# A GRU over 128 steps on one core: a one-column product of zeros ahead of two kinds of products, weight loads at most two at a time, r's biases after all of r's products, and one block's weight sums moved forward

## The chip, the core and the metric

The kernel runs on one core of a Trainium2 chip, in one launch. Its engines: TensorE (PE, with its weight loads listed apart as PEld), VectorE (DVE), ScalarE (ACT), GpSimd (POOL) and SyncE (SP), which here only issues DMAs. The metric is the device time of one execution in microseconds (us), the median over the runs; lower is better. All data are float32, except where a tile is called bfloat16.

## The reference

`x` is (64, 128, 512), 64 sequences of 128 steps of 512 features; the initial state is `cond_1024` (64, 512). Each gate has a weight of 1024 x 512 (the upper half for x, the lower for the state) and a bias.

```python
do_prop = ((t + 1) % 4 == 0) & (t < T - 1)
def step(h, inp):
    x_t, prop = inp
    comb = jnp.concatenate([x_t, h], axis=-1)
    z = jax.nn.sigmoid(comb @ Wz + bz)
    r = jax.nn.sigmoid(comb @ Wr + br)
    comb2 = jnp.concatenate([x_t, r * h], axis=-1)
    h_cand = jnp.tanh(comb2 @ Wh + bh)
    h_new = (1.0 - z) * h + z * h_cand
    h_next = jnp.where(prop, jnp.tanh(h_new @ Wp + bp), h_new)
    return (h_next, h_new)
_, ys = jax.lax.scan(step, h0, (xs, do_prop))
return x + transpose(ys)
```

So each step has a candidate product (with `r * h`), and after every fourth step but the last the state goes through one more product, called the projection here.

## The kernel before, in words

**Tiles.** The 64 sequences are two lanes of 32 (`h` = 0 and 1, `S` = 2, `V` = 32). The 512 features are four chunks of 128; PE's array is used as four column groups of 32 columns (`part(q)`, q = 0 to 3), each with the 32 sequences of a lane as its weights. `four_tiles` (L279) issues one product on each of the four groups; a product with all 512 features is four of them, 16 instructions ("x16" in the profile). The moving data are the weights of the network, 128 columns (or 192 in the products on x).

**Two kinds of work on PE.** The recurrent products of step t need the state of step t-1: the r and z gates (`wrz`, L279, lines with bank_B<-wrz,ht or bank_A<-tr,ht), then the candidate (`wc`), then, after every fourth step, the projection (`wp`). The products on x (`wx`, L708) need no state. They are done for four steps at a time (a group), by a scheme that replaces eight block products by seven, blocks 1 to 7, made of sums of weights and of inputs; the sums of weights (`sums_w`) are made once, at the start. The units of these products are put by `fill` between the recurrent ones, so that PE has work while DVE and ACT compute the gates. All of it is in an order written out ahead, engine by engine; each engine does its instructions in that order and waits at each for the semaphores of what it reads.

**A step's chain.** r's products on PE, sigmoid on ACT (L1031, bank_A), `r * h` on DVE (L1146), its transposition on DVE (L275, tile `rhT`), the candidate's products on PE into bank_B (lane 0) and bank_C (lane 1), tanh on ACT, the new state on DVE (L1263, L1264). ACT has copied the x part into the bank ahead of the candidate's products (`seed_h`, L1007), and the bias `bp` ahead of the projection's (L1152). So the first product of a candidate waits for two engines: DVE for rhT, ACT for the bank.

**The start.** SP issues, in this order: x of steps 0 and 1, the x half of r's weight in three parts (`load_wx`, L162), x of step 2, the x halves of z's and the candidate's weight in two parts each (L162), then, in `later_loads`, the recurrent weights of r and z (`load_w`, L141, tile `wrz`), x of step 3 and of group 1, `wc`, x again, and after that `wp`. POOL issues the loads of the biases (tile `stage`) and of the initial state (cond). The first three steps' products on x are done plainly (`plain_gate`), with the biases as small bfloat16 products (`bias_products`, L600, from `thirds`, the three bfloat16 parts of the biases, which DVE makes in L229 to L234). Before there is data, PE runs products on zeros (`idle`, L259). DVE joins and transposes x into xT (L353), later sums the recurrent weights (L972). POOL makes the sums of weights of blocks 4 to 7 by `sum_inner` (L307 and L312, tiles sums_w and wx), one task for each block, after a first sum called "left".

The places that the change touches, cut to their core:

```python
for ks in (range(0, 1), range(1, 2), range(2, K)):
    for t in range(2):
        plain_gate(t, R, ks, bias=ks[-1] == K - 1)
later_loads()
join_x(0, 2)
plain_gate(2, R, range(K), bias=True)
...
for i in (6, 5, 4, 7):
    task(f"inner{i}", lambda i=i: [sum_inner(i, Gp), sum_left(i, Gp)], "left")
```

Of the kernel before, what the change touches and what calls it, by code (L numbers as in the profile page):

```python
# [10 lines left out]
BF16 = mybir.dt.bfloat16  # L11
# [7 lines left out]
def kernel(  # L19
# [14 lines left out]
    nc = tc.nc  # L34
    B, T, D = x.shape
    H = h0.shape[1]
    P = 128
    S = 2
    V = B // S
    NQ = P // V  # L40
    J = H // NQ
    U = J // 2
    C = 2
    K = D // P
# [4 lines left out]
    R, Z, H_ = range(3)  # L49
    assert V * NQ == P and D == H and J == P and T % 8 == 0  # L50

    const = ctx.enter_context(tc.tile_pool(name="const", bufs=1))
# [4 lines left out]
    ctx.enter_context(tc.manual_schedule())  # L57


    zeros = two.tile([P, 4 * J], BF16, tag="e_sb", name="zeros")  # L60
    nc.vector.memset(zeros, 0.0)
    ident = const.tile([3 * V, 3 * V], F32, name="ident")
# [10 lines left out]
    wx = const.tile([P, K, 3, H], F32, name="wx")  # L73
# [18 lines left out]
    gates_in = (Wr, Wz, Wh)  # L92
# [12 lines left out]
    def part(q):  # L105
        return slice(q * V, (q + 1) * V)
# [9 lines left out]
    row = (bank["B"], bank["C"])  # L116
# [7 lines left out]
    def load_x(tile_, t0, n, later=None):  # L124
        for h in range(S):
            for q in (0, 2, 1, 3):
# [9 lines left out]
                else:  # L136
                    later.append(run)

    def load_w(wt, w):
        for k0 in (0, 2):  # L140
            nc.sync.dma_start(  # L141
                out=wt[:, k0 : k0 + 2, :],
                in_=w.rearrange("(p k) n -> p k n", k=K)[:, k0 : k0 + 2],
            )

    both_queues = (nc.sync, nc.scalar)
# [12 lines left out]
            )  # L159

    def load_wx(i, k0, k1):
        nc.sync.dma_start(  # L162
            out=wx[:, k0:k1, i, :],
            in_=gates_in[i][:D].rearrange("(p k) n -> p k n", k=K)[:, k0:k1],
        )

    lands = {}
# [34 lines left out]
    for h in range(S):  # L202
        nc.gpsimd.dma_start(
            out=h_rows[:, h, :],
            in_=h0[ts(h, V), :].rearrange("b (q j) -> q b j", q=NQ),
# [62 lines left out]
    def plain_order(v):  # L268
        return v.rearrange("p (e k) -> p k e", k=K)

    def state_order(v):
        return v.rearrange("p (k e) -> p k e", k=K)
# [4 lines left out]
    def four_tiles(region, left, rhs, start=False):  # L277
        for q in range(NQ):
            nc.tensor.matmul(  # L279
                region[part(q)],  # L280
                lhsT=left,
                rhs=rhs(q),
                start=start,
                stop=True,
                skip_group_check=True,
            )


    def tick(ns):
        nonlocal clock  # L290
        clock += ns
# [223 lines left out]
    def flush(pending, late=0, most=99):  # L515
        n = 0
        while pending and n < most:
            b, j = pending.pop(0)
            n += 1
            late += 560  # L520
            b.out(j)
            b.out_at[j] = clock + late
            if b.finished():
                flying.remove(b)
                did.add(b.name)
        poll()
        return n
# [14 lines left out]
    def fill(n, eager=False, soon=True):  # L542
        nonlocal doing, owed
        drip(DRIP)
        n, owed = n + owed, 0
        while n > 0:
            if queue:
                unit, cost, end = queue.pop(0)
                unit()
                tick(cost * UNIT)  # L550
                n -= cost
                if end is not None:
                    end()
                poll()
                continue
            if doing is None:
                best = pick()
                if best is None or best[0] > clock + 400:
                    owed = n
                    return  # L560
                b, j = best[1:]
                b.left.remove(j)
                doing = b, j, b.units(j)
            b, j, us = doing
            us.pop(0)()
            tick(UNIT)
            n -= 1
            if not us:
                doing = None
                b.made_at[j] = clock  # L570
                (at_dve if j in (3, 7) else at_act).append((b, j))
                if soon:
                    flush(at_act, 300)
                    if eager:
                        flush(at_dve, 300)

    def x_left(t, h, k):
        g, j = divmod(t, Q4)
        c0, s0 = divmod(k, C)
        return xT[g][:, j][:, c0, s0 * B + h * V : s0 * B + (h + 1) * V]  # L580

    def plain_bank(t, h):
        return row[h] if t == 0 else xb[2 * (t % 2 if t > 3 else t == 2) + h]

    def plain_gate(t, i, ks, bias=False):
        for h in range(S):
            region = plain_bank(t, h)[:, ts(i, J)]
            for k in ks:
                four_tiles(
                    region,  # L590
                    x_left(t, h, k),
                    lambda q: wx[:, k, i, ts(q, J)],
                    i == R and k == 0,
                )
            if bias:
                bias_products(region, slice(i, i + 1))

    def bias_products(region, which):
        for q in range(NQ):
            nc.tensor.matmul(  # L600
                region[part(q)],
                lhsT=picks[:, q],
                rhs=thirds[:, which],
                start=False,
                stop=True,
                skip_group_check=True,
            )
# [220 lines left out]
    def poll():  # L828
        again = True
        while again:  # L830
            again = False
            for n, (name, run, after, step) in enumerate(todo):
                if steps_done >= step and all(a in did for a in after):
                    del todo[n]
                    run()
                    did.add(name)
                    again = True
                    break
# [135 lines left out]
    def first_sums(v):  # L974
        turn(ht[:, A11 : A12 + 1].rearrange("p n v -> p (n v)"), v)
# [29 lines left out]
    def seed_h(t, lane, h):  # L1005
        have_sums(t)
        nc.scalar.copy(  # L1007
            row[lane][:, 2 * J : 3 * J].rearrange("p (n u) -> p n u", n=C), G[t][:, h, :, H_]
        )
# [8 lines left out]
    PLAIN = T - 4  # L1018
# [54 lines left out]
    def full(region, lT, w):  # L1073
        for k in range(K):
            four_tiles(region, lT[:, ts(k, V)], lambda q: w[:, k, ts(q, J)])
# [13 lines left out]
    }  # L1089

    def tile_(tag, t, pool=one):
        return pool.tile([P, S, J], F32, tag=tag, name=f"{tag}_{t}")

# [41 lines left out]
    def step(t, h_old, v_1):  # L1135
# [73 lines left out]
        if last:  # L1209
# [5 lines left out]
            for h in range(S):  # L1215
                nc.vector.scalar_tensor_tensor(
                    out=kept[:, h], in0=z_[:, h], scalar=1.0, in1=h_h[:, h],
# [6 lines left out]
        else:  # L1224
            nc.vector.scalar_tensor_tensor(
                out=keep, in0=z_ps, scalar=1.0, in1=h_old, op0=ALU.subtract, op1=ALU.mult
# [19 lines left out]
        def candidate(h):  # L1246
            region = row[h][:, 2 * J : 3 * J]
            full(region, rhT[:, h], wc)
            tick(FULL)
            c, z_h = cand[:, h], z_ps[:, h]  # L1250
            if last:
                nc.scalar.activation(c, region, AF.Tanh)
                nc.vector.tensor_mul(z_h, c, z_h)
                o = xr[g][:, j, h, :]
                nc.vector.tensor_add(o, z_h, o)
                for q in (0, 2, 1, 3):
                    way = both_queues[q // 2] if h else nc.sync
                    way.dma_start(out=out[ts(h, V), t, ts(q, J)], in_=o[part(q)])
                return
            nc.scalar.activation(state_order(c), plain_order(region), AF.Tanh)  # L1260
            if t + 1 < T and not prop:
                seed_h(t + 1, h, h)
            nc.vector.tensor_mul(z_h, c, z_h)  # L1263
            nc.vector.tensor_sub(h_new[:, h], z_h, keep[:, h])  # L1264

        candidate(0)
        if prop:
            pT = tile_("rhT", f"{t}p")
# [17 lines left out]
        for h in range(S):  # L1286
            fill(next(places), eager)
            flush(at_act, 300)
            full(row[h][:, :J], pT[:, h], wp)
            tick(FULL)  # L1290
            nc.scalar.activation(state_order(h_next[:, h]), plain_order(row[h][:, :J]), AF.Tanh)
            seed_h(t + 1, h, h)
            if h == 0:
                flush(at_dve, 300, 1) or join_next()
                first_sums(h_next[:, 0])
                join_next() or flush(at_dve, 1000, 1)
            else:
                second_turn(h_next[:, 1])
# [35 lines left out]
    idle(4)  # L1334
    for ks in (range(0, 1), range(1, 2), range(2, K)):
        for t in range(2):
            plain_gate(t, R, ks, bias=ks[-1] == K - 1)
    later_loads()
    join_x(0, 2)
    plain_gate(2, R, range(K), bias=True)  # L1340
    spread(bank["E"], slice(0, 2))
    spread(bank["A"], slice(2, 3))
    h_init = tile_("h", "init", two)
# [35 lines left out]
    task("raw12_1", lambda: sum_raw12(1), ("join", 1, 0), ("join", 1, 1))  # L1379
    task("left", lambda: [sum_outer_1(Gp), did.add("outer1")], "plain3")  # L1380
    task("raw34_1", lambda: sum_raw34(1), ("join", 1, 2), ("join", 1, 3))
    for i in (6, 5, 4, 7):
        task(f"inner{i}", lambda i=i: [sum_inner(i, Gp), sum_left(i, Gp)], "left")

    def pair(a, p1, p2, n):
# [27 lines left out]
    h, v_1 = h_init, None  # L1413
    for t in range(T):
        if t == 1:
            load_group(3)
        h, v_1 = step(t, h, v_1)
# [39 lines left out]
```

## Time and profile before

| | |
|---|---|
| runs | 1255.95 us median of 3 (1255.64 to 1255.97) |
| the profiled execution | 1254.05 us, its span 1252.3 us |
| PE busy | 1224.6 us, 98% of the span, 37576 instructions |
| DVE, ACT, POOL busy | 901.9, 683.9, 916.5 us |
| PE busy from 60 to 1200 us | 1131.88 us of 1140.00 |
| PE busy from 5 to 60 us | 47.23 us of 55.00 |

The span runs from the first to the last thing that the profiler recorded; the execution's time holds a little besides. A line such as "139.99 0.41 PEld L279 LDWEIGHTS bank_B<-wc,rhT ... x16 [0.16 <-ACT bank_A L1031]" gives the start, the length, the engine and line of a run of like instructions, and in brackets how long the engine had been idle before it and what ended that. Where an instruction waits for two engines, one alone is named. Rows of stretches give the length, then the busy time (and count) of PE, PEld, DVE, ACT and POOL, the granted TensorE clock (1.00 is full, 0.50 half), the DMA engines' busy share and GB/s.

### The profile page before, as it was taken

To read this page: it belongs to the slowest core of one execution; us is meant where nothing else is said; L and a number is where in the kernel's file an instruction comes from. 1 tells how busy PE (TensorE), PEld (TensorE's weight loads), DVE (VectorE), ACT (ScalarE), POOL (GpSimd) and SP (SyncE) were. 2 spreads that over 40 slices of the span, in tenths; PEclk is the share of its full clock that TensorE was granted. 3 is DMA by queue.
4 is the path that set the end of the run, shared out by engine and by line. 5 is a ranking of instruction groups with operands and counts; after the bars stand their busy time and mean duration, and the time that the engine had idled before them with its cause. 6 is when DMAs were issued, how large, how long until landed. Compare 5 with 4: busy or idle time off the path is not lost.

```text
span 1252.3 us, 84837 instructions
## 1 busy us (share of the span) xinstructions
PE 1224.6 (98%) x37576; PEld 1121.4 (90%) x37576; DVE 901.9 (72%) x2964; ACT 683.9 (55%) x2086; POOL 916.5 (73%) x1046
## 2 busy tenths in 40 slices
PE   7999999999999999999999999999999999999987
PEld 6789999999999999989889999998899999999977
DVE  5667777777777777777767777777777777777664
ACT  1345555555555555555555565555555555555554
POOL 1698686877868778686876868778687786868751
PEclk8999999999999999999999999999999999999999
DMA  7203222212222112222212221212222122222111
GB/s 241 82 17 74 52 53 57 54 48 51 56 57 56 46 49 54 57 52 54 53 47 50 53 65 47 59 46 50 57 54 49 50 55 56 52 57 51 50 48 48
DMA packets 98686, 72.26 MB, mean 58 GB/s; under 512 B 13028, under 2 KB 94576, under 8 KB 98320
## 3 DMA queue, kind: packets, MB, share of 16 engines
q1 hardware_dynamic: 97888, 66.54, 20.8%
q8 instruction: 295, 4.83, 1.6%
q14 instruction: 71, 0.58, 0.2%
q0 software_dynamic: 256, 0.14, 0.0%
q10 hardware_dynamic: 176, 0.16, 0.0%
HBM read 25.63 MB, written 16.78 MB: 34 GB/s over the span
## 4 chain that ended last, share of the span: by engine, by line
PE 94%; issue 1%; POOL 1%; DVE 1%; ACT 1%; DMA 0%; DVEq 0%; POOLq 0%; ACTq 0%
PE x L708 39%; PE bank_B L279 20%; PE bank_C L279 15%; PE bank_A L279 13%; PE bank_E L279 5%; PE x L279 2%; DMA stage<-in_L_cond_bh_dram 0%; POOL wx L312 0%; POOL sums_w L312 0%; ACT bank_A L1031 0%; POOL sums_w L307 0%; DVE xT L353 0%; DVE wrz L972 0%; POOL stage L193 0%; ACT gx L819 0%
## 5 line engine op out<-in xcount | busy, mean ns | idle before, releaser
L307 POOL TENSOR_TENSOR mb<-mb,mb 128x768 f32<-128x768 f32 x167 | 304.8, 1833 | 168.6 <-ACT mb L752 74.8
L708 PE MATMUL x<-sums_w,s 128*32 128x192 f32 x2880 | 178.5, 326 | 0.0
L307 POOL TENSOR_TENSOR xr<-xr,h 128x256 f32<-128x256 f32 x127 | 111.0, 874 | 83.1 <-DMA xr<-in_x_dram 48.0
L279 PE MATMUL bank_B<-wrz,ht 128*32 128x128 f32 x4000 | 168.3, 273 | 2.5 <-issue 1.7
L279 PE MATMUL bank_A<-tr,ht 128*32 128x128 f32 x3936 | 163.7, 273 | 0.5 <-DVE bank_B L1182 0.5
L279 PE MATMUL bank_B<-wc,rhT 128*32 128x128 f32 x4096 | 139.5, 274 | 3.0 <-ACT bank_B L1152 0.5
L279 PE MATMUL bank_C<-wc,rhT 128*32 128x128 f32 x4096 | 139.4, 273 | 0.1
L279 PEld LDWEIGHTS bank_B<-wrz,ht 128*32 128x32 f32 x4000 | 128.7, 110 | 10.4 <-issue 6.4
L279 PEld LDWEIGHTS bank_B<-wc,rhT 128*32 128x32 f32 x4096 | 110.4, 109 | 25.3 <-ACT bank_A L1031 20.3
L279 PEld LDWEIGHTS bank_A<-tr,ht 128*32 128x32 f32 x3936 | 124.9, 110 | 8.0 <-DVE bank_B L1182 4.8
L819 ACT COPY gx<-mb 64x384 f32<-64x384 f32 x248 | 126.4, 510 | 3.0
L708 PE MATMUL x<-sums_w,o 128*32 128x192 f32 x1920 | 121.3, 326 | 1.2 <-issue 1.2
L279 PEld LDWEIGHTS bank_C<-wc,rhT 128*32 128x32 f32 x4096 | 118.5, 110 | 0.3 <-ACT bank_C L1152 0.3
L708 PEld LDWEIGHTS x<-sums_w,s 128*32 128x32 f32 x2880 | 106.0, 110 | 5.7
L1189 DVE TENSOR_TENSOR bank_C<-bank_A,gx 128x256 f32<-128x256 f32 x123 | 53.2, 432 | 72.9 <-PE bank_A L279 72.9
L1146 DVE TENSOR_TENSOR rh<-bank_A,h 128x128 f32<-128x128 f32 x192 | 56.0, 292 | 50.0 <-ACT bank_A L1031 43.3
L738 ACT COPY x<-x 128x384 f32<-128x384 f32 x108 | 49.9, 462 | 76.4 <-PE x L708 76.4
L307 POOL TENSOR_TENSOR mb<-mb 128x768 f32<-128x768 f32 x47 | 86.3, 1835 | 2.5
L1031 ACT ACTIVATE bank_A<-bank_B 128x128 f32<-128x128 f32 x123 | 32.2, 262 | 102.2 <-DVE bank_C L1189 99.6
L275 DVE STREAM_TRANSPOSE rhT<-rh 128x128 f32<-128x128 f32 x256 | 79.8, 312 | 9.0
L1264 DVE TENSOR_TENSOR h<-bank_E,keep 128x128 f32<-128x128 f32 x254 | 74.1, 292 | 15.2
L752 ACT COPY mb<-x 128x384 f32<-128x384 f32 x108 | 51.7, 479 | 57.4 <-PE x L708 53.8
(884 smaller groups left out, 3100.1 us busy)
## 6 DMA issues: line engine op xcount, KB each, us to landing
gx<-mb SPq DMA_DIRECT2D x248, 96.0 KB, 2.2
xr<-in_x_dram SPq DMA_DIRECT2D x248, 64.0 KB, 2.9
out_dram<-xr SPq DMA_DIRECT2D x248, 64.0 KB, 1.8
wx<-in_L_cond_Wz_dram SPq DMA_DIRECT2D x2, 512.0 KB, 6.0
wx<-in_L_cond_Wh_dram SPq DMA_DIRECT2D x2, 512.0 KB, 7.1
wrz<-in_L_cond_Wr_dram SPq DMA_DIRECT2D x2, 512.0 KB, 9.4
wrz<-in_L_cond_Wz_dram SPq DMA_DIRECT2D x2, 512.0 KB, 9.6
wc<-in_L_cond_Wh_dram SPq DMA_DIRECT2D x2, 512.0 KB, 5.7
```

The source lines that it names most:

```text
L275: nc.vector.transpose(out=dst, in_=src)
L279: nc.tensor.matmul(region[part(q)], lhsT=left, rhs=rhs(q), start=start, stop=True, skip_group_check=True,)
L307: nc.gpsimd.tensor_add(o, a, b)
L708: nc.tensor.matmul(v[part(2 * h + c)], lhsT=left[:, ts(h, V)], rhs=right[:, c::2], start=j in (1, 5) and m == 0 and n == 0, stop=True, ski ...
L738: nc.scalar.copy(self.a, self.u)
L752: nc.scalar.copy(self.block(1, 0), runs(self.u))
L819: (ready, lambda h=h: (nc.scalar.copy(to(h, h), of(h, h)), one_done(clock + 1000)))
L1031: nc.scalar.activation(gate_out(dst), gate_in(lane, i), AF.Sigmoid)
L1146: nc.vector.tensor_mul(rh[:, h], r_ps[:, h], h_old[:, h])
L1189: nc.vector.tensor_add(row[1][:, : 2 * J].rearrange("p (n j) -> p n j", n=2), bcast(u_ps), G[t][:, 1, :, :2].rearrange("p n g u -> p n (g ...
L1264: nc.vector.tensor_sub(h_new[:, h], z_h, keep[:, h])
```

## The change

Four edits:

1. A tile `nil` of zeros (bfloat16, 128 x 34) is set once. `touch(v)` issues a product of it, with one moving column, on column group 0, added to what is in the bank (`start=False`), so that it changes nothing there. It stands ahead of the candidate's first product in steps 1 to T-5 (123 times) and ahead of the projection's first product (31 times).
2. `paced` stands in place of the plain DMA issue in `load_w` and `load_wx`: from the third weight load on, SP first issues an instruction that does nothing but read what the load before last writes, so that it waits for that load's landing. The DMAs of x are issued as before, but in the same queue.
3. r's biases, so far added after r's products of each of steps 0, 1 and 2, are added after r's products of all three.
4. The sums of weights of block 5 come ahead of those of block 6.

```diff
+    nil = const.tile([P, V + 2], BF16, name="nil")
+    nc.vector.memset(nil, 0.0)
...
+    loading = []
+
+    def paced(to, src):
+        if len(loading) > 1:
+            nc.sync.keepalive_nop(ins=[nc.sync.lower_ap(loading[-2])], hint="paced")
+        nc.sync.dma_start(out=to, in_=src)
+        loading.append(to)
...
     def load_w(wt, w):
         for k0 in (0, 2):
-            nc.sync.dma_start(
-                out=wt[:, k0 : k0 + 2, :],
-                in_=w.rearrange("(p k) n -> p k n", k=K)[:, k0 : k0 + 2],
+            paced(
+                wt[:, k0 : k0 + 2, :],
+                w.rearrange("(p k) n -> p k n", k=K)[:, k0 : k0 + 2],
             )
...
     def load_wx(i, k0, k1):
-        nc.sync.dma_start(
-            out=wx[:, k0:k1, i, :],
-            in_=gates_in[i][:D].rearrange("(p k) n -> p k n", k=K)[:, k0:k1],
+        paced(
+            wx[:, k0:k1, i, :],
+            gates_in[i][:D].rearrange("(p k) n -> p k n", k=K)[:, k0:k1],
         )
...
+    def touch(v):
+        nc.tensor.matmul(
+            v[part(0), :1], lhsT=nil[:, :V], rhs=nil[:, V : V + 1], start=False, stop=True,
+            skip_group_check=True,
+        )
...
+        if 0 < t < PLAIN:
+            touch(row[0][:, 2 * J : 3 * J])
         candidate(0)
...
+            if h == 0:
+                touch(row[0][:, :J])
             full(row[h][:, :J], pT[:, h], wp)
...
     for ks in (range(0, 1), range(1, 2), range(2, K)):
         for t in range(2):
-            plain_gate(t, R, ks, bias=ks[-1] == K - 1)
+            plain_gate(t, R, ks)
     later_loads()
     join_x(0, 2)
-    plain_gate(2, R, range(K), bias=True)
+    plain_gate(2, R, range(K))
+    for t in range(3):
+        plain_gate(t, R, (), bias=True)
...
-    for i in (6, 5, 4, 7):
+    for i in (5, 6, 4, 7):
```

The order of instructions at the places concerned follows, each row one instruction or a run of like ones ("x7"), with the semaphores that it waits for in brackets. Lines of the changed kernel are numbered 11 higher (L290 is L279 there), and the buffers' numbers differ.

PE at the candidate of one step, before: the products on x end, then come the candidate's for lane 0 (bank_B) and lane 1 (bank_C).

```order
L708 MATMUL x_103<-sums_w,s_4_2914 32x192 [waits Activation_49,Pool_49]
L708 MATMUL x_103<-sums_w,s_4_2914 32x192 x3
L279 MATMUL bank_B<-wc,rhT_3299 32x128 [waits DVE_49,Activation_49]
L279 MATMUL bank_B<-wc,rhT_3299 32x128 x15
L279 MATMUL bank_C<-wc,rhT_3299 32x128 [waits DVE_49,Activation_49]
L279 MATMUL bank_C<-wc,rhT_3299 32x128 x15
```

The same place after.

```order
L719 MATMUL x_105<-sums_w,s_4_2940 32x192 [waits Activation_49,Pool_49]
L719 MATMUL x_105<-sums_w,s_4_2940 32x192 x3
L1104 LDWEIGHTS nil
L1104 MATMUL bank_B<-nil 32x1 [waits Activation_49]
L290 MATMUL bank_B<-wc,rhT_3328 32x128 [waits DVE_49]
L290 MATMUL bank_B<-wc,rhT_3328 32x128 x15
L290 MATMUL bank_C<-wc,rhT_3328 32x128 [waits DVE_49,Activation_49]
L290 MATMUL bank_C<-wc,rhT_3328 32x128 x15
```

The wait for ACT has gone from the candidate's first product to the product of zeros; lane 1 keeps its two.

PE in the start, at the last part of r's products for steps 0 (bank_B, bank_C) and 1 (x_102), before: the biases (`thirds` by `picks`, which wait for DVE) stand between them.

```order
L279 MATMUL bank_B<-wx,xT_158 32x128 [waits DMAHW4_49]
L279 MATMUL bank_B<-wx,xT_158 32x128 x7
L600 LDWEIGHTS picks
L600 MATMUL bank_B<-thirds,picks 32x128 [waits DVE_49]
...
L279 MATMUL bank_C<-wx,xT_158 32x128 x8
L600 LDWEIGHTS picks
L600 MATMUL bank_C<-thirds,picks 32x128
...
L279 MATMUL x_102<-wx,xT_158 32x128 x8
```

After: step 0's banks, step 1's (x_104, x_105) and step 2's (x_106, x_107) come first, then the biases.

```order
L290 MATMUL bank_B<-wx,xT_165 32x128 x7
L290 MATMUL bank_C<-wx,xT_165 32x128 x8
L290 MATMUL x_104<-wx,xT_165 32x128 x8
L290 MATMUL x_105<-wx,xT_165 32x128 x8
L290 MATMUL x_106<-wx,xT_165 32x128 [waits DVE_49]
L290 MATMUL x_106<-wx,xT_165 32x128 x15
L290 MATMUL x_107<-wx,xT_165 32x128 x16
L611 LDWEIGHTS picks
L611 MATMUL bank_B<-thirds,picks 32x128
```

Between r's products of step 1 and the biases now stand 32 products of step 2, whose first waits for DVE (xT of step 2).

POOL at the sums of weights, before: block 6 (four rows on sums_w alone), then block 5 (those with wx).

```order
L312 TENSOR_TENSOR sums_w<-sums_w 128x384
L307 TENSOR_TENSOR sums_w<-sums_w 128x384
L312 TENSOR_TENSOR sums_w<-sums_w 128x384
L312 TENSOR_TENSOR sums_w<-sums_w 128x12x32
L312 TENSOR_TENSOR sums_w<-wx 128x384
L307 TENSOR_TENSOR sums_w<-sums_w,wx 128x384
L312 TENSOR_TENSOR sums_w<-wx,sums_w 128x384
L312 TENSOR_TENSOR wx<-wx 128x4x3x32
```

After, the two fours have changed places, and nothing else on POOL.

```order
L323 TENSOR_TENSOR sums_w<-wx 128x384
L318 TENSOR_TENSOR sums_w<-sums_w,wx 128x384
L323 TENSOR_TENSOR sums_w<-wx,sums_w 128x384
L323 TENSOR_TENSOR wx<-wx 128x4x3x32
L323 TENSOR_TENSOR sums_w<-sums_w 128x384
L318 TENSOR_TENSOR sums_w<-sums_w 128x384
L323 TENSOR_TENSOR sums_w<-sums_w 128x384
L323 TENSOR_TENSOR sums_w<-sums_w 128x12x32
```

SP in the start, after: an instruction that waits stands ahead of each weight load from the third on, and the DMAs behind it in the queue wait with it; before, these rows are the same without the NO_OPs.

```order
L147 DMA wx<-in_L_cond_Wr_dram 128x512 x2
L146 NO_OP [waits DMAHW2_49]
L147 DMA wx<-in_L_cond_Wr_dram 128x2x512
L168 DMA xr_109<-in_x_dram 32x2x128 x3
L168 DMA xr_109<-in_x_dram 32x2x128 [waits DMAHW0_49]
L146 NO_OP [waits DMAHW3_49]
L147 DMA wx<-in_L_cond_Wz_dram 128x2x512 [waits DMAHW1_49]
L146 NO_OP [waits DMAHW4_49]
L147 DMA wx<-in_L_cond_Wz_dram 128x2x512 [waits DMAHW2_49]
```

## The prediction

> **What bounds the kernel now.** I read the page's busy line first, then the busy time by stretches, the chain that ended last, the waits, and the instructions in order of time at the places where the change lies. The stretches are cut where the granted clock changes.
>
> ```profile
> PE 1224.6 (98%) x37576; PEld 1121.4 (90%) x37576; DVE 901.9 (72%) x2964; ACT 683.9 (55%) x2086; POOL 916.5 (73%) x1046
> ...
> 8.18:11.59 3.41, 1.41 (x48) 0.95 (x40) 2.54 (x7) 0.00 (x0) 1.95 (x3) 1.00 1.00 307
> 11.59:15.00 3.41, 3.41 (x76) 3.30 (x79) 0.60 (x1) 0.00 (x0) 0.00 (x0) 0.50 0.96 326
> ...
> 18.42:21.83 3.41, 1.35 (x51) 1.08 (x43) 3.18 (x10) 0.30 (x1) 0.68 (x1) 1.00 0.98 316
> 21.83:25.24 3.41, 3.41 (x80) 3.37 (x75) 3.24 (x9) 0.00 (x0) 0.00 (x0) 0.50 0.28 76
> ...
> 55.63:57.28 1.65, 0.00 (x1) 0.00 (x0) 1.42 (x6) 0.48 (x1) 1.65 (x3) 1.00 0.00 0
> ...
> 60.00:1200.00 1140.00, 1131.88 (x34876) 1040.39 (x34868) 834.33 (x2776) 645.53 (x1963) 875.75 (x999) 1.00 0.21 52
> ```
>
> The first time in each row after the length is PE's busy time, and the number after the five engines is its clock. Between 60 and 1200 us PE is idle for 8.1 us of 1140: the recurrence is bound by PE, and whatever PE is given there or spared there is the time. The only places where much time lies idle are the start and the end. In the start PE loses 2.0 us in the row that begins at 8.18, then runs a whole row of 3.41 us at half clock (1.7 us lost); it loses 2.06 us in the row at 18.42 and again a row at half clock (1.7 us); and it stands still for 1.65 us at 55.63. What ended these waits:
>
> ```profile
> PE x L279 <- issue: 2.1, 1, 2.1
> PE bank_B L600 <- DVE thirds L234: 1.7, 1, 1.7
> PE x L708 <- POOL wx L312: 1.6, 1, 1.6
> PEld bank_B L279 <- ACT bank_A L1031: 20.3, 89, 0.5
> ```
>
> The 1.7 is the r biases waiting for the split of the biases on DVE; the 1.6 is block 5's sum on POOL; the 2.1 has no semaphore behind it (the run of products stops midway), so I take it to be PE's own instructions arriving late. The last row is the weight load of the candidate's first product, late 89 times.
>
> **The product of zeros.** How long the load takes after what it waits for, in one step where it is just late, in one where it is very late, and for a load with one wait alone (bank_C):
>
> ```profile
> 139.56 0.31 DVE L275 STREAM_TRANSPOSE rhT<-rh 128x128 f32<-128x128 f32 x1
> 139.99 0.41 PEld L279 LDWEIGHTS bank_B<-wc,rhT 128*32 128x32 f32 x16 [0.16 <-ACT bank_A L1031]
> 140.02 0.54 PE L279 MATMUL bank_B<-wc,rhT 128*32 128x128 f32 x12
> ...
> 649.50 0.43 DVE L1189 TENSOR_TENSOR bank_C<-bank_A,gx 128x256 f32<-128x256 f32 x1 [0.90 <-PE bank_A L279]
> ...
> 649.99 0.38 PEld L279 LDWEIGHTS bank_C<-tr,ht 128*32 128x32 f32 x16 [0.17 <-DVE bank_C L1189]
> ...
> 650.65 0.31 DVE L275 STREAM_TRANSPOSE rhT<-rh 128x128 f32<-128x128 f32 x1
> ...
> 651.07 0.84 PEld L279 LDWEIGHTS bank_B<-wc,rhT 128*32 128x32 f32 x32 [0.49 <-ACT bank_A L1031]
> 651.10 1.08 PE L279 MATMUL bank_B<-wc,rhT 128*32 128x128 f32 x32
> ```
>
> With two waits (DVE and ACT) the load starts 0.11 to 0.12 us after the transposition ends (139.87 to 139.99, 650.96 to 651.07); with one it starts 0.06 after (649.93 to 649.99). The zero product takes the ACT wait, so the candidate's load keeps one: 0.05 us sooner. What that is worth stands in the chain:
>
> ```profile
> by line: PE x L708 42.4%; PE bank_B L279 21.1%; PE bank_C L279 16.0%; PE bank_A L279 13.8%; PE bank_E L279 4.9%; issue 0.8%; ACT bank_A L1031 0.4%; DVE xT L353 0.1%; ACT gx L819 0.1%; POOL wx L312 0.1%; DVE rhT_3p L275 0.1%; DVE h L1264 0.1
> ...
> 119.53 0.27 ACT bank_A L1031
> ...
> 602.56 0.90 PE bank_B L279 x32
> 603.46 0.87 PE bank_C L279 x32
> ...
> 1179.05 0.27 ACT bank_A L1031
> ```
>
> The first row is the chain of the stretch from 57 to 1200 us by line: ACT bank_A is 0.4% of 1143 us at 0.27 us a time, some 16 steps (119.53 the first shown, 1179.05 the last) in which PE stands idle for rhT, and there 0.05 us each is gained: 0.8 us. In the other 73 late steps the candidate's 32 passes take 0.90 us where the second lane's take 0.87: 0.03 us each, 2.2 us in all, is the most that is to be had.
>
> Against that stands the price of 154 zero products (123 candidates, 31 projections). No row shows one alone. Lower end nothing: its load and its pass hide behind the products before it. Upper end a full set of four bfloat16 products on all four column groups: 0.48 + 0.02 us in the rows below for 16 float32 and 4 bfloat16 passes, less 0.44 for 16, that is 0.06 us. Nearest is the reload that it forces: its weights stand in column group 0, so the candidate's load for that group can begin only when the product has run, and load to product is 0.03 us (651.07 to 651.10). I take 0.03, and nothing in the 16 idle steps.
>
> ```profile
> 25.66 0.48 PE x L279 x15
> 26.14 0.02 PE x L600 x2
> ...
> 58.79 0.44 PE bank_A L279 x16
> ```
>
> So: 16 steps gain 0.05 (-0.8 us), 73 change 0.03 for 0.03 (0), the other 65 pay 0.03 (+2.0): **+1.2 us**. Ends: free, -0.8 - 2.2 = -3.0 us; a whole set, 138 x 0.06 - 3.0 = +5.3 us.
>
> **The start: r's biases and the paced loads.**
>
> ```profile
> 8.87 0.35 DVE L229 CAST thirds<-stage 4x384 bf16<-4x384 f32 x1 [2.87 <-DMA stage<-in_L_cond_bh_dram]
> 9.25 0.64 PE L279 MATMUL bank_B<-wx,xT 128*32 128x128 f32 x16 [0.32 <-DMA wx<-in_L_cond_Wr_dram]
> 11.55 0.64 DVE L353 STREAM_TRANSPOSE xT<-xr 128x256 f32<-128x256 f32 x1
> 11.57 0.30 PE L600 MATMUL bank_B<-thirds,picks 96*32 96x128 bf16 x4 [1.68 <-DVE thirds L234]
> ...
> 39.03 1.23 DVE L972 TENSOR_TENSOR wrz<-wrz 128x1024 f32<-128x1024 f32 x1 [2.31 <-PE bank_C L279]
> ```
>
> With the biases moved, PE goes on at 9.25 with the r products of steps 0 and 1, 64 passes, 1.75 us at 0.44 for 16, to 11.0; then step 2's, whose xT stands on DVE behind the split and ends at 12.19, or earlier if the biases land sooner. Of the 2.0 us idle and the 1.7 us of half clock (3.7 together) I leave 1.2: up to 1.2 us of waiting for xT or for Wr's last part, whose load now waits for the first part. That is **-2.5 us**; bounds -3.7 and -0.5.
>
> The pacing adds 13 waits to SP's queue, each ahead of a weight load; behind them stand the x loads of steps 2 to 11, the recurrent weights and bp.
>
> ```profile
> stage<-in_cond_dram POOLq DMA_DIRECT2D x2, 64.0 KB, 7.4
> wrz<-in_L_cond_Wz_dram SPq DMA_DIRECT2D x2, 512.0 KB, 9.6
> wp<-in_L_cond_Wp_dram SPq DMA_DIRECT2D x2, 512.0 KB, 5.5
> ```
>
> Queued eight deep, a load takes up to 9.6 us to land and the DMA engines are full (a share of 0.96 to 1.00 in the first three rows quoted); with two in flight the instruction fetches and the initial state (7.4 us for 64 KB) should be served sooner. Of 2.06 + 1.7 us at 18.42 I take half, **-1.9 us** (bounds 0 and -3.8). For PE to come 4.4 us sooner, DVE must too: it has 2.3 us idle ahead of the sum at 39.03 (waiting for PE), and the other 2.1 must come from an earlier initial state, on which its chain of work hangs; if that fails the start gives 2.3.
>
> Both half-clock rows follow a row in which PE was idle for 2.0 to 2.06 us of 3.41; the sum takes the one for the cause of the other. The Trainium skill, "TensorE: Matmul & The Clock Gate", Part 1 on the clock gate, says that the clock goes down after at least one idle window of about 3.4 us. By that rule 2.0 us of idle would not do it, and the two rows would have another cause (rival F); the trace speaks against it, both times.
>
> **Block 5's sums sooner.** POOL does the sums of blocks 6, 5, 4, 7 in turn:
>
> ```profile
> 48.70 1.32 POOL L312 TENSOR_TENSOR sums_w<-sums_w 128x384 f32<-128x384 f32 x1
> ...
> 53.09 1.02 POOL L312 TENSOR_TENSOR sums_w<-wx 128x384 f32<-128x384 f32 x1
> ...
> 57.28 0.86 PE L708 MATMUL x<-wx,s12r 128*32 128x192 f32 x16 [1.65 <-POOL wx L312]
> ```
>
> Block 6 begins at 48.70, block 5 at 53.09. First in line, block 5 is done 4.4 us sooner, 2.8 us before PE asks at 55.63: **-1.65 us**, all of it. Block 6 is then done when block 5 was, ahead of the second group's first batch; nothing is late next. The added memset of 34 columns on DVE lies under the loads: 0.
>
> **Sum**: -2.5 - 1.9 - 1.65 + 1.2 = -4.8 us against the span of 1252.3. That execution took 1254.05 us and the three runs' median is 1255.95; the difference goes on the median: 1251.1 us.
>
> **Rivals.** (B) The zero product costs a whole set: +5.3 for +1.2, so -0.7, 1255.2 us. For it: products that run alone on one group are nowhere in the trace; against it: one column. (C) It costs nothing, -3.0: 1246.9 us. (D) The start does not do what it is meant to: the fetch stall stays and DVE's sums begin no sooner, so that PE only waits later (DVE is busy 3.18 and 3.24 us of 3.41 in the rows at 18.42 and 21.83); block 5's gain stays: -1.65 + 1.2, 1255.5 us. (E) Two loads in flight are too few, and it ends slower: wp's pair takes 5.5 us to land; at 2.75 a load, eight loads from Wr's last (9.2) to the last of wrz end at 31, 4 us after DVE wants them in the forecast, and group 1's x stands behind them. It decides from about 2.3 us a load. Less the 2.3 us of DVE's slack, with the zero products, block 5's gain lost in it, +2 to +6: 1260 us. Against it: wp's pair had x loads ahead of it. (F) The half clock does not follow from the waits, and comes at its time in any case: about 1 us each from the two waits and block 5's 1.65, less 1.2, -2.5 in all, 1253.4 us. Against it: a row at half clock stands behind each of the two idle rows and nowhere else. It is what the clock rule of the Trainium skill named above would give.
>
> **Numbers.** A difference under 0.2% (2.5 us) can't be told from none here. Forecast 0.50 (from -2.6 to -7), B 0.13, C 0.11, D 0.15, E 0.09, F 0.02. Faster: 0.50 + 0.11 + half of F = 0.62; same: B, D, a fifth of E and half of F = 0.31; slower 0.07. The range 1246.5 to 1256.5 leaves out E, half of C and the tails.
>
> **What would show it.** In the changed profile: no wait for thirds near 10 us and no half-clock row after it; the one at 20 us gone or shorter; no wait of PE on POOL wx near 55; the candidate's load 0.06 us after rhT; PE busy from 60 to 1200 us longer or shorter by what the zero products cost. I am wrong if PE's passes around them stretch by more than 0.03, or if weights of wrz or x of group 1 are waited for.

## The result, and the profile after

The changed kernel takes 1241.61 us, median of 4 runs (1239.39 to 1243.68), against 1255.8 us (1254.21 to 1255.97, 4 runs): ratio 0.9881, 95% interval 0.986 to 0.9902. In runs made later it was 1239.23 against 1252.38 us, ratio 0.9897 (0.9877 to 0.9917). The forecast was 1251.1, range 1246.5 to 1256.5: the direction was right, the gain some three times too small, and the range missed it.

The head of the page after, and then its busy time in two stretches (length, PE, PEld, DVE, ACT, POOL, granted clock, DMA share, GB/s):

```profile
span 1240.3 us, 85008 instructions
PE 1218.3 (98%) x37730; PEld 1092.4 (88%) x37730; DVE 902.2 (73%) x2965; ACT 684.0 (55%) x2086; POOL 917.6 (74%) x1046
```

```profile
5.00:60.00 55.00, 45.35 (x1339) 38.27 (x1342) 37.41 (x85) 12.16 (x36) 21.75 (x26) 1.00 0.59 171
60.00:1200.00 1140.00, 1138.33 (x35374) 1025.55 (x35363) 843.13 (x2804) 652.45 (x1984) 883.65 (x1005) 1.00 0.23 53
```

From 60 to 1200 us PE is idle for 1.7 us where it was 8.1. From 5 to 60 us it is busy for 45.35 us, before for 47.23, and now at full clock throughout. The transposition rhT of lane 0 marks the steps; here are those of steps 2 and 123, before and then after:

```profile
66.19 0.31 DVE L275 STREAM_TRANSPOSE rhT<-rh 128x128 f32<-128x128 f32 x1
...
1218.36 0.31 DVE L275 STREAM_TRANSPOSE rhT<-rh 128x128 f32<-128x128 f32 x1
```

```profile
65.84 0.31 DVE L286 STREAM_TRANSPOSE rhT<-rh 128x128 f32<-128x128 f32 x1
...
1205.08 0.31 DVE L286 STREAM_TRANSPOSE rhT<-rh 128x128 f32<-128x128 f32 x1
```

So in these two executions the whole start, in which the forecast had put its gain, gives 0.35 us by step 2; steps 2 to 123 give 1152.17 - 1139.24 = 12.9 us; the end gives 1.3 back. The gain is in the recurrence, and the chain of waits from 57 to 1200 us, by line, names what went:

```profile
by line: PE x L719 42.5%; PE bank_B L290 21.5%; PE bank_C L290 16.1%; PE bank_A L290 13.9%; PE bank_E L290 5.0%; issue 0.2%; ACT gx L830 0.1%; DVE xT L364 0.1%; ACT mb L763 0.1%; DVE rhT_3p L286 0.1%; DVE h L1282 0.1%; ACT bank_A L1042 0.0%
```

"issue" is 0.2% where it was 0.8%, "ACT bank_A" 0.0% where it was 0.4%. Issue is time in which PE waits for nothing that the profile shows. One such place before, in order of time:

```profile
634.71 0.42 PE L279 MATMUL bank_A<-wrz,ht 128*32 128x128 f32 x7
636.02 0.49 PE L279 MATMUL bank_A<-wrz,ht 128*32 128x128 f32 x9 [0.89 <-issue]
```

A run of like products stops between its seventh and its eighth. The trace's records explain where. PE's instructions (weight loads, products and semaphore instructions, in order) are loaded by DMA in packets of 16 KB on a queue of their own, 295 of them for 75682 recorded instructions, one for each 256. All 19 gaps of 0.24 us or more without a semaphore wait between 57 and 1205 us before lie ahead of an instruction whose number leaves 193 when divided by 256, and each ends 1.3 to 1.6 us after the end of such a packet (here it ran from 633.14 to 634.57, and PE goes on at 636.02). So PE waits there for the next block of its program. Summed over the places numbered so (the time from the start of the instruction ahead to the one there, where over 0.125 us, less 0.027), the stalls of steps 2 to 123 are **13.7 us before and 2.3 us after**: 11.4 of the 12.9.

The time from PE's crossing into a block (the instruction with that number) to the start of the next packet, called the fetch's delay below, is 0.92 us in the mean before and 0.78 after. Near the candidate (from a tenth of a step ahead of rhT to a tenth behind it) it is 1.2 to 1.5 before, 0.8 after.

### The profile page after: what moved, and what is told of

Read it like the earlier page. It is cut to its first block, busy times and chain, and to the rows that moved or that the text cites. A ratio compares the mean times of both kernels' runs of the same rounds, so it can differ in the third digit from the quotient of the medians.

```text
span 1240.3 us, 85008 instructions
## 1 busy us (share of the span) xinstructions
PE 1218.3 (98%) x37730; PEld 1092.4 (88%) x37730; DVE 902.2 (73%) x2965; ACT 684.0 (55%) x2086; POOL 917.6 (74%) x1046
## 4 chain that ended last, share of the span: by engine, by line
PE 93%; DMA 3%; SPq 1%; DVE 1%; ACT 1%; issue 0%; DVEq 0%; ACTq 0%
PE x L719 39%; PE bank_B L290 20%; PE bank_C L290 15%; PE bank_A L290 13%; PE bank_E L290 5%; PE x L290 1%; DMA wx<-in_L_cond_Wr_dram 1%; DMA wc<-in_L_cond_Wh_dram 1%; SPq L132 1%; DMA wx<-in_L_cond_Wh_dram 1%; DMA wx<-in_L_cond_Wz_dram 0%; DMA wp<-in_L_cond_Wp_dram 0%; DMA wrz<-in_L_cond_Wr_dram 0%; DMA xr<-in_x_dram 0%; DVE xT L364 0%
## 5 line engine op out<-in xcount | busy, mean ns | idle before, releaser
L719 PE MATMUL x<-sums_w,s 128*32 128x192 f32 x2880 | 172.3, 326 | 0.1
L290 PE MATMUL bank_B<-wrz,ht 128*32 128x128 f32 x4000 | 158.8, 273 | 2.1 <-issue 1.3
L290 PE MATMUL bank_A<-tr,ht 128*32 128x128 f32 x3936 | 155.6, 273 | 0.5 <-DVE bank_B L1200 0.5
L290 PE MATMUL bank_B<-wc,rhT 128*32 128x128 f32 x4096 | 137.5, 273 | 0.7
L290 PE MATMUL bank_C<-wc,rhT 128*32 128x128 f32 x4096 | 137.1, 273 | 0.1
L290 PEld LDWEIGHTS bank_B<-wrz,ht 128*32 128x32 f32 x4000 | 119.1, 110 | 12.8 <-issue 5.8
L290 PEld LDWEIGHTS bank_A<-tr,ht 128*32 128x32 f32 x3936 | 116.6, 110 | 10.5 <-DVE bank_B L1200 4.3
L290 PEld LDWEIGHTS bank_B<-wc,rhT 128*32 128x32 f32 x4096 | 113.1, 110 | 7.3 <-DVE rhT L286 6.0
L290 PEld LDWEIGHTS bank_C<-wc,rhT 128*32 128x32 f32 x4096 | 115.8, 110 | 0.5 <-ACT bank_C L1170 0.3
L719 PE MATMUL x<-sums_w,o 128*32 128x192 f32 x1920 | 116.2, 326 | 0.0
L719 PEld LDWEIGHTS x<-sums_w,s 128*32 128x32 f32 x2880 | 94.4, 110 | 14.4 <-issue 0.2
L364 DVE STREAM_TRANSPOSE xT<-xr 128x256 f32<-128x256 f32 x126 | 82.4, 659 | 6.6 <-DMA xr<-in_x_dram 4.7
L1282 DVE TENSOR_TENSOR h<-bank_E,keep 128x128 f32<-128x128 f32 x254 | 74.1, 292 | 15.6 <-DVE bank_E L1281 0.5
```

The lines of the kernel that those rows point to most:

```text
L290: nc.tensor.matmul(region[part(q)], lhsT=left, rhs=rhs(q), start=start, stop=True, skip_group_check=True,)
L364: nc.vector.transpose(out=xT[g][:, i].rearrange("p c (a h b) -> p h (c a) b", a=S, h=S), in_=src[:, i].rearrange("p h (e k) -> p h k e", k=K),
L719: nc.tensor.matmul(v[part(2 * h + c)], lhsT=left[:, ts(h, V)], rhs=right[:, c::2], start=j in (1, 5) and m == 0 and n == 0, stop=True, ski ...
```

## The experiments

The theories: **R**, the sequencer: a product that waits for two semaphores has a semaphore instruction ahead of it, and while PE's sequencer stands at it the next fetch is not asked for; the product of zeros takes one of the two waits, the semaphore instruction goes (524 rows with two waits in PE's order before, 372 after), and the sequencer runs ahead. **P**, position: 156 instructions more move the blocks' boundaries past the transfers. **S**, start: the paced loads and the rest of the start brought it. All times stand beside runs of the kernel before on the same chip.

| kernel | median us | ratio to before (95%) | stalls, steps 2-123, us | fetch's delay, us |
|---|---|---|---|---|
| before | 1252.3 to 1258.5 | 1 | 13.7 | 0.92 |
| after | 1241.61 | 0.9881 (0.986-0.9902) | 2.3 | 0.78 |
| e1 zero products only | 1239.59 | 0.9902 (0.988-0.9925) | 2.0 | 0.67 |
| e2 start only | 1252.2 | 1.0001 (0.9984-1.0017) | 15.6 | 0.99 |
| e3 behind | 1252.32 | 1.0002 (0.9982-1.0021) | 13.8 | 1.00 |
| e4 unpaced | 1239.88 | 0.9898 (0.9874-0.9921) | 1.9 | 0.69 |
| e5 two waits | 1260.94 | 1.0073 (1.0052-1.0095) | 11.3 | 0.96 |
| e6 double | 1243.58 | 0.9932 (0.9911-0.9953) | 2.3 | 0.73 |
| e7 early | 1248.82 | 0.9969 (0.9953-0.9986) | 2.3 | 0.67 |
| e8 more | 1244.71 | 0.994 (0.992-0.9959) | 2.3 | 0.62 |
| e13 candidates only | 1240.89 | 0.9912 (0.9892-0.9931) | 2.2 | 0.73 |
| e14 projections only | 1251.19 | 0.999 (0.9975-1.0006) | 11.3 | 0.96 |

Before's medians are those of four later sets of runs; the last two columns are of one profiled execution each. The kernel of e1 was profiled once more as e9: stalls 2.6, a delay larger by some 0.07. So differences of that size between rows tell nothing.

**e1 and e2: the change in two.** e1 is before with the product of zeros at both places and nothing else:

```diff
+        if 0 < t < PLAIN:
+            touch(row[0][:, 2 * J : 3 * J])
         candidate(0)
...
+            if h == 0:
+                touch(row[0][:, :J])
             full(row[h][:, :J], pT[:, h], wp)
```

> Before plus the 154 zero products alone. In the trace of after, PE's stalls at every 256th of its instructions (the 193rd of each 256) fell from 13.7 to 2.3 us between steps 2 and 123. Theory P (position): the 156 instructions more in PE's stream move those places past the transfers; then this kernel has after's stalls and before's start: 1242 to 1245 us. Theory R (sequencer): the zero product removes the semaphore instruction that two waits need, PE's sequencer runs ahead and asks for its next instructions sooner: 1242 to 1245 as well. Theory S (start): the paced loads and the rest of the start's edits brought it: 1254 to 1257 us here, stalls as before.

e2 is the changed kernel without these lines.

> After without the zero products: paced loads, r's biases later, block 5's sums sooner. P and R: the stalls are before's, the start gains the 0.4 us that the traces show by step 2: 1254.5 to 1256.5 us. S: 1242 to 1245 us.

Measured: e1 has the whole gain (1239.59), e2 none (1252.2). S is out.

**e3: as many instructions, no wait taken.** In `candidate`, behind the products of lane 0, and at the projection likewise:

```diff
             full(region, rhT[:, h], wc)
+            if h == 0 and 0 < t < PLAIN and t % 2 == 0:
+                touch(region)
...
             full(row[h][:, :J], pT[:, h], wp)
+            if h == 0 and t % 8 == 3:
+                touch(row[0][:, :J])
```

> Before with 77 zero products that stand behind the candidate's 16 products of lane 0 in every second step, and behind the projection's in every second one: 154 instructions more in PE's stream, nearly as many as after has, but no wait is taken off any product, all two-wait products stay. P: the stalls fall as in after, 1243 to 1248 us. R: the stalls stay at 10 us or more, 1253 to 1257 us. S: 1255 to 1257 us.

Measured: 1252.32 us, stalls 13.8. P is out as the cause: 154 instructions more change nothing while the semaphore instructions stay. The other kernels don't sort by their number of instructions either: against before, PE's stream has 113 to 464 more in those with few stalls (e7, e13, e1, e8, e6), and 0, 32, 154 and 616 more in those with many (e2, e14, e3, e5).

**e5: the same place, with both waits.** The zero product has rhT as its weights, so it waits for DVE as well as for ACT:

```diff
-            v[part(0), :1], lhsT=nil[:, :V], rhs=nil[:, V : V + 1], start=False, stop=True,
+            v[part(0), :1], lhsT=lT[:, :V], rhs=nil[:, :1], start=False, stop=True,
...
+            touch(row[0][:, 2 * J : 3 * J], rhT[:, 0])
```

> The zero products stand where they stood in e1, but each multiplies a float32 column of zeros by rhT itself, so that it has both waits (ACT and DVE) and the semaphore instruction with them; the candidate's own products have none left. Theory R (the semaphore instruction of two waits holds PE's sequencer, and with it the next fetch): the stalls are before's, 10 us or more, and the time 1253 to 1258 us. Rival N (a product of any kind ahead of the candidate brings it): stalls near 2 us, 1240 to 1243 us.

Measured: 1260.94 us, slower than before, stalls 11.3. That is 2.9 us over the top of R's range; what is over lies outside the stalls (steps 2 to 123 less their stalls take 1145.7 us, before 1138.5), most likely in the float32 zero products, each of two passes. The same rows, the chain of waits from 57 to 1200 us by line, of e3 and of e5 (in both "issue" and the wait behind ACT bank_A stay as before), and of e1:

```profile
by line: PE x L710 42.2%; PE bank_B L281 20.8%; PE bank_C L281 16.1%; PE bank_A L281 13.7%; PE bank_E L281 4.9%; issue 0.8%; ACT bank_A L1033 0.4%; DVE xT L355 0.1%; POOL sums_w L309 0.1%; ACT gx L821 0.1%; DVE mb L750 0.1%; POOL sums_w L31
```

```profile
by line: PE x L710 42.0%; PE bank_B L281 21.6%; PE bank_C L281 16.0%; PE bank_A L281 13.8%; PE bank_E L281 4.9%; issue 0.7%; ACT bank_A L1033 0.4%; PE bank_B L1095 0.3%; ACT gx L821 0.1%; ACT mb L748 0.0%; ACT x L740 0.0%; ACT h_3p L1304 0.
```

```profile
by line: PE x L710 42.3%; PE bank_B L281 21.4%; PE bank_C L281 16.1%; PE bank_A L281 13.9%; PE bank_E L281 5.0%; issue 0.2%; ACT gx L821 0.1%; DVE xT L355 0.1%; ACT mb L754 0.1%; DVE mb L752 0.1%; DVE rhT_3p L277 0.1%; DVE h L1273 0.1%; ACT
```

**e13 and e14: which of the semaphore instructions.** e1 without the second edit, and without the first.

> Before plus the zero products ahead of the candidates only (123; 122 two-wait semaphore instructions gone). Theory R with 'held' (only those count at which PE is held): stalls near 2 us, 1239 to 1241.5 us. Rival C (all count alike): four fifths of the gain, about 1242 to 1244.

> Before plus the zero products ahead of the projections only (31; 30 semaphore instructions gone). R with 'held': no projection is held, so the stalls stay at 10 us or more, and the time is that of before within 2 us. Rival C: a fifth of 12 us, 2.4 us faster than before.

Measured: 1240.89 (stalls 2.2) and 1251.19 (11.3). The chain's rows from 57 to 1200 us, e13 and then e14:

```profile
by line: PE x L710 42.3%; PE bank_B L281 21.4%; PE bank_C L281 16.0%; PE bank_A L281 14.0%; PE bank_E L281 5.0%; issue 0.2%; ACT gx L821 0.1%; DVE xT L355 0.1%; ACT mb L754 0.1%; DVE mb L752 0.1%; DVE rhT_3p L277 0.1%; DVE h L1273 0.1%; ACT
```

```profile
by line: PE x L710 42.4%; PE bank_B L281 21.3%; PE bank_C L281 16.0%; PE bank_A L281 13.8%; PE bank_E L281 4.9%; issue 0.7%; ACT bank_A L1033 0.3%; DVE xT L355 0.1%; ACT gx L821 0.1%; DVE rhT_3p L277 0.1%; DVE h L1273 0.1%; ACT mb L748 0.0%
```

The candidates have the whole gain, as far as can be told, the projections nothing that can be told. These two alone don't put rival C out: its 2.4 us lie within e14's interval, and e14's 11.3 us of stalls within the 11.3 to 15.6 of the kernels that keep all their semaphore instructions. But e13 keeps 30 of them more than e1 and has its few stalls, and e8 below takes away 153 more and saves none. That points to the semaphore instructions at which PE is held, those of the candidates, whose weight load is late in 89 steps (PE itself stands idle for it in 18 of steps 2 to 122), and not to their number.

**e8: lane 1 too.** e1 with a zero product ahead of `candidate(1)` and of the projection's second lane.

> e1 with zero products ahead of lane 1's candidate (123 more) and projection (31 more) too, which takes 153 of the remaining 372 two-wait semaphore instructions away. R: the fetches start sooner again and the stalls of 2.0 us between steps 2 and 123 go below 1 us; against that the price of 154 more, 2 us: 1239 to 1241.5 us. Rival P2 (e1's fewer stalls were the place of the blocks after all): stalls anywhere from 0 to 13 us.

Measured: 1244.71; the stalls are 2.3 us, not below 1, and only the price is seen. The fetch's delay is 0.62 for e1's 0.67, which can't be told apart. That is a miss for R as it was written; it fits only with 'held' added, as in e13 and e14: where PE is not held, the instruction shows no cost in stalls.

**e6 and e7: the price of a zero product.** e6 issues each twice. e7 issues it ahead of the units of products on x that stand before the candidate:

```diff
+        if 0 < t < PLAIN:
+            touch(row[0][:, 2 * J : 3 * J])
         fill(next(places), eager)
         flush(at_act, 300)
```

> e1 with each zero product issued twice. Its price alone: by the prediction's value, 0.03 us each, 154 more cost up to 4.6 us where nothing waits, 1243 to 1244.5; by its upper end, 0.06, 9 us; by the step lengths of after's trace (an ordinary step 0.012 us longer than before) about 2 us, 1241 to 1242.5 us. Theory R expects the stalls at 2 us as in e1.

> e1 with each zero product ahead of the products on x that stand before the candidate (or projection), so that the wait for ACT lies some products earlier; no semaphore instruction at the candidate. R: stalls at 2 us or less, and the candidate's load has no reload behind it: 1238 to 1240 us. If ACT is not done by then, PE waits there and it ends at 1243 us or more. Rival N (it must stand directly ahead of the candidate): 1250 us or more.

Measured: e6 takes 1243.58 us, 4.0 above e1 (on another chip; before's medians there are within 0.3); its steps 2 to 123 less the stalls take 1139.97 us, e1's 1136.56, so 3.4 us for 154 more, **0.022 us each**. e3 gives (1140.26 - 1138.45)/77 = 0.024, e8 (1140.80 - 1136.56)/154 = 0.028. e7 keeps the few stalls, as R has it, but takes 1248.82 us, 9 more than expected. Its trace shows two losses. There the zero product stands behind bank_C's products. At 90 places, where ACT had been done for over 5 us, it starts a median 0.061 us late, 6.2 us in all; in e1, behind products on x, it starts on time but for some 15 places. Products on x have 192 columns and a set of four takes 0.163 us, those of bank_C 128 and 0.109 us; that the longer set covers the extra weight load is the likely reason, and wasn't tested. At the 31 projections ACT is not done, as the expectation allowed: the zero product starts 0.05 us after ACT's copy of `bp` ends, and at 15 of those up to 1200 us that is 0.36 us late, 5.4 us in all. In half of that PE shows as idle:

```profile
PE bank_B L1095 <- ACT bank_B L1161: 2.7, 15, 0.2
```

Part of both is won back at the candidates: from the last product ahead of them to their first it is 18.1 us in all, in e1 22.5.

**e4 and e9 to e12: the start.** e4 is after without the two lines in `paced` that issue the waiting instruction; e9 is e1 again, and e10, e11 and e12 add one edit of the start each to it.

> After without the waits of SP between the weight loads. In after the first candidate stands 3.4 us later than before, with wrz's last part landing at 31.5 us for 23.2. If that is the pacing, the start gains 3 us: 1237.5 to 1239.5 us against after's 1241.6, by P and by R. By S (the pacing is what freed the instruction fetches) it goes back to 1250 us or more. If the half clock comes back without the pacing, 1241 to 1243 us.

> e1 (before plus the zero products) once more, as the base of the three that follow: with few stalls left, its runs spread over 2.6 us where before's spread over 12, so that the start's edits can be seen on it. 1238.5 to 1241 us.

> e9 plus r's biases later. By the prediction's sum: 2.5 us less than e9 (bounds 0.5 and 3.7), about 1237. Rival: the next instruction fetch, at 16 to 20 us, is what PE waits for there whatever came before, and it gives back what was gained: within 0.6 us of e9.

> e9 plus block 5's sums ahead of block 6's. By the prediction: 1.65 us less than e9, 1238 (e1's trace shows the wait of PE on POOL wx, 1.6 us, unchanged from before). Rival: another wait takes its place (POOL's next sums, or the first group's joins): within 0.6 us of e9.

> e9 plus the paced weight loads. By the prediction: 1.9 us less than e9 (bounds 0 and 3.8), 1237.7. Rival E: two loads in flight are too few, wrz's last part lands at 31 us for 22.5 and wc's at 42 for 32, and it ends 1 to 4 us slower than e9, 1240.5 to 1243.5.

Measured: e4 1239.88, 0.4 over its range; it can't be told apart from e1 or from the changed kernel, and S's 1250 is out once more. Run together, e9 1240.61 (1237.78 to 1243.92), e10 1240.64 (1238.69 to 1242.2), e11 1238.32 (1237.47 to 1240.47), e12 1240.96 (1240.36 to 1242.54). The base spreads over 6 us, not 2.6 as expected, so that about 1 us is the least that these medians can tell. What PE waits for from 4 to 62 us (total, times, longest), of e9 and then of e10, e11, e12:

```profile
PE x L281 <- issue: 3.7, 2, 2.8
PE x L710 <- POOL wx L314: 1.7, 1, 1.7
PE bank_B L602 <- DVE thirds L236: 1.6, 1, 1.6
```

```profile
PE x L281 <- issue: 5.1, 2, 3.5
PE x L710 <- POOL wx L314: 1.6, 1, 1.6
PE bank_B L281 <- DMA wx<-in_L_cond_Wr_dram: 1.2, 1, 1.2
```

```profile
PE x L281 <- issue: 3.6, 2, 3.1
PE bank_B L281 <- issue: 1.9, 1, 1.9
PE bank_B L281 <- DMA wx<-in_L_cond_Wr_dram: 1.0, 1, 1.0
```

```profile
PE bank_C L290 <- ACT bank_A L1038: 2.6, 1, 2.6
PE x L290 <- DVE xT L364: 2.3, 2, 1.9
PE bank_B L290 <- DMA wx<-in_L_cond_Wr_dram: 2.2, 1, 2.2
PE bank_B L290 <- issue: 0.4, 1, 0.4
```

With r's biases later (e10) the wait for thirds is gone and the wait for instructions is 1.4 us longer, besides 1.2 for Wr. Its longest piece ends at the same time in both, behind a packet that runs from 18.13 to 19.25 us in e9 and from 18.11 to 19.22 in e10, though PE gets to that place 0.75 us sooner in e10 (16.86 us for 17.61):

```profile
20.71 1.22 PE L281 MATMUL x<-wx,xT 128*32 128x128 f32 x17 [2.83 <-issue]
```

```profile
20.59 0.71 PE L281 MATMUL x<-wx,xT 128*32 128x128 f32 x17 [3.46 <-issue]
```

With block 5 first (e11) the wait for POOL wx is gone; from rhT of step 1 to that of step 2 it is 13.81 us (50.28 to 64.09), in e9 15.29 (49.23 to 64.52). With paced loads (e12) the stall for instructions is gone from this list's head, and in its place PE waits for r's weights and for the first step's gates.

**e15 and e16: a better version?** e15 is e13 with block 5 first, e16 the changed kernel once more.

> e13 plus block 5's sums ahead of block 6's. If both hold, 1.5 to 2.3 us less than e13: 1237 to 1239.5, and below the changed kernel of the same call by 1 to 4 us. If the projections' zero products count, no better than the changed kernel.

> The changed kernel as it is, for the comparison with e13 and e15 in one call: 1240 to 1243 us.

Measured: 1238.22 us (ratio 0.9894, 0.9872 to 0.9915) against 1239.23 (0.9897). It does with two edits, one of them at the candidates alone, what the changed kernel does; that it is faster can't be told. Against e13 it takes 2.7 us less, as e11 took 2.3 less than e9.

## Why the prediction was wrong, by its own steps

**The bound.** "PE is idle for 8.1 us of 1140 [...] whatever PE is given there or spared there is the time" holds. The step that failed comes behind it: those 8.1 us, and the "issue 0.8%" in the chain row quoted there (9 us), got no term; after, they are 1.7 us and 0.2%. I had taken the 2.1 us stop in the start for instructions that arrive late, and did not ask whether the same cause stands in the recurrence, nor whether the product of zeros touches it. So no rival held a result below 1246.9.

**The product of zeros: +1.2 forecast, 12 to 13 measured the other way** (e1: 0.9902 of 1252.59 is 12.3 us less). The terms that I did name were near. Its price was put at 0.03 us; a second one costs 0.022 (e6), and with the first, an ordinary step is 0.010 to 0.012 us longer in e1 than before. The load's wait was to fall by 0.05 us; here is a candidate after, in order of time:

```profile
139.06 0.31 DVE L286 STREAM_TRANSPOSE rhT<-rh 128x128 f32<-128x128 f32 x1
139.34 0.10 PEld L1104 LDWEIGHTS <-nil 128*32 128x32 bf16 x1
139.43 0.88 PEld L290 LDWEIGHTS bank_B<-wc,rhT 128*32 128x32 f32 x32
139.51 0.17 PE L1104 MATMUL bank_B<-nil 128*32 128x1 bf16 x1
139.51 1.06 PE L290 MATMUL bank_B<-wc,rhT 128*32 128x128 f32 x32
```

rhT ends at 139.37 and the load starts 0.06 later (0.12 before); but from load to product it is now 0.08, for 0.03 before, since the zero product stands between. In the 18 steps in which PE stands idle for rhT, the zero product has run by then: the candidate's first product starts 0.055 us after the transposition's end, 0.147 before, and the step is some 0.05 us shorter. All that together, steps 2 to 123 less the stalls, is 1.9 us faster (1138.45 to 1136.56); 1.5 of it lies in the 29 steps that held a stall before, so that some 0.4 is left for the terms of the forecast, which had put them at +1.2, from -3.0 to +5.3. What was missing is the other effect of the same edit: 11.8 us of stalls less (13.7 to 2.0).

**r's biases: -2.5 forecast, 0.0 measured** (e10 against e9). The wait went, as said. The row at half clock behind it, 1.7 us of the term, doesn't stand in e9's profile either (its one such row begins at 20.55 us, e10's at 21.37), so that there was less to be had there. What the term left out is the stall for instructions some us later: its packet lands at the same time, 19.2 us, with and without the edit, and PE goes on at 20.6 to 20.7.

**Paced loads: -1.9 forecast, +0.35 measured** (e12). The stalls for instructions do shrink: the issue rows from 4 to 62 us come to 0.4 us in e12 and 3.9 in e9, so the mechanism was there. In the changed kernel, where r's biases move too, they come to 2.9 us, before to 3.0. Rival E's price came with it. In after, the loads of wrz land at 23.70 to 31.54 us (before 18.64 to 23.22) and wc's at 40.70 and 41.94 (31.11 and 32.56), and PE waits 3.24 us for the first step's gates (2.6 in e12). The two about cancel. The bounds, 0 and 3.8, had no loss on their side: that was wrong, since E stood beside them.

**Block 5 sooner: -1.65 forecast, -2.3 measured** (e11, medians whose ranges overlap; e15 against e13 gives -2.7), 1.5 by the step's length in the profile. Right, and the one edit of the start that pays. Since e2, all three together, is 1.0001 (0.9984 to 1.0017), the -6.05 forecast for them came out as nothing that can be told from 2 us either way.

**Rivals.** B and C held the price of the product apart, and the measurement lies between the value taken and C. D comes nearest to what the start did: in e10 the fetch stall stays and DVE's last sum of wrz begins at 37.94 us, in e9 at 37.28. That DVE's own load was the reason, as D had it, isn't shown. F: the half clock does follow from the waits (below), and F is out.

## What to carry to other kernels

Where an engine is nearly full, read "issue" in the chain as a term of its own and look for its places: a run of like instructions that stops midway, again and again at the same number modulo a block, is an engine waiting for its program. A product that waits late for two semaphores cost more here than its own 0.05 us; taking one of the two waits on a tiny instruction ahead of it was worth 1%, all of it, as far as can be told, at the products where the engine was really held. Each term of a start's sum should say which wait ends next, since two of the three edits of the start removed or shortened their wait and gave the time to the next one.

## What was not expected of the hardware

- **The instruction stream.** A packet of 16 KB carries 256 of PE's instructions and takes 0.9 to 2.2 us; where PE waits for it in the kernel before, it goes on 1.3 to 1.6 us after the packet's end. Crossing to start takes up to 2.9 us there. A block lasts 3.7 to 5.1 us without a stall, so the fetch is just in time. How the sequencer asks for a block is not in the trace. That a held semaphore instruction delays the request is the reading that e3, e5, e13 and e14 leave, not something seen.
- **The half clock.** In all 18 profiles, in the first 60 us, a row of 3.41 us at half clock follows each of the 17 stretches of 3.41 us (counted on the grid of the clock's own changes) in which PE was idle for 2.00 us or more, and none of those with 1.89 or less. Two neighbours of that limit, before and then e6, each with the row behind it:

```profile
8.18:11.59 3.41, 1.41 (x48) 0.95 (x40) 2.54 (x7) 0.00 (x0) 1.95 (x3) 1.00 1.00 307
11.59:15.00 3.41, 3.41 (x76) 3.30 (x79) 0.60 (x1) 0.00 (x0) 0.00 (x0) 0.50 0.96 326
```

```profile
16.18:19.59 3.41, 1.52 (x54) 1.25 (x45) 2.31 (x7) 0.96 (x3) 1.00 (x1) 1.00 1.05 381
19.59:23.01 3.42, 2.48 (x100) 2.48 (x103) 3.21 (x10) 0.00 (x0) 0.00 (x0) 1.00 0.63 157
```

After's wait of 3.24 us (36.1 to 39.4) falls on two stretches, 1.75 us idle in the first and 1.49 in the second, and the clock stays at 1.00. The Trainium skill ("TensorE: Matmul & The Clock Gate", Part 1) asks for a whole idle window; here 2.0 us of idle time in a stretch of 3.41 was enough, and the measurement decides.
